# A recurrent token-mixing block on one core: square roots by ln and exp, the sigmoid by tanh, two activation tables set by the program, and a new written order

## The chip, the core and the metric

The kernel runs on one core of a Trainium2 chip. Its matrix engine is called TensorE (PE in the profile), the engine for element-wise work and scans VectorE (DVE), the one for activation functions ScalarE (ACT), the general one GpSimd (POOL); SyncE (SP) issues most transfers. ScalarE evaluates its functions from a loaded table; a function of another set of tables needs an ACT_TABLE_LOAD first. The metric is device time in microseconds, the median over runs.

## What is computed

x has 8 batches of 256 tokens with 512 channels, ctx holds the state. Shortened:

```python
xn = ln(x); sx = shift(xn) - xn                 # layer norm, token shift
xxx = tanh((xn + sx * maa_x) @ maa_w1)          # five groups of 32
x5 = xn + sx * (maa_stack + xxx @ maa_w2)       # mixes for k, w, v, r, g
w = exp(-exp(time_decay + tanh(x5[1] @ decay_w1) @ decay_w2))
r, k, v = x5[3] @ Wr.T, x5[0] @ Wk.T, x5[2] @ Wv.T
g = silu(x5[4] @ Wg.T)
# scan over tokens, 32 heads of 16 x 16:  out = r (u k v + s);  s = k v + w s
att = head_norm(out) * gn_w + gn_b              # (a - mean) * rsqrt(var + eps) per head
x = x + (att * g) @ Wo.T
xn2 = ln(x); sx2 = shift(xn2) - xn2
rr = sigmoid((xn2 + sx2 * ffn_maa_r) @ ffn_Wr.T)
kk = square(relu((xn2 + sx2 * ffn_maa_k) @ ffn_Wk.T))
x = x + rr * (kk @ ffn_Wv.T)
```

All data are float32.

## The kernel before

The program is a list of small operations, each noted with its engine, a duration, and the buffers it reads and writes (`Plan.add`). For every batch there are three stages: `inputs_of_scan` (layer norm, mixes, the products for k, w, v, r, g), `scan` (four blocks of 128 channels; each block's v is written to DRAM and read back spread over 16 rows per head, 512 KB a tile, by SP), and `rest` (head norm, gate, the Wo product, second layer norm, the two feed-forward products with weights streamed anew for each batch). Three batches are under way at a time, in different stages.

`Plan.order` sets the order of work. It takes the operations by rank from a table of numbers written out by hand (`TURNS`, one row per stage), assigns buffers from small pools as they become free, and reckons a start for each operation from the noted durations (`TAKES`, `LANDS`, `LATENCY`, `SWITCH`); the operations are then emitted sorted by these starts. Each engine works through its own part of that order strictly in sequence, and so does SP with its transfers. The PSUM pool `ps` has six buffers; `wrep`, one more, holds the decay spread out for the scans.

Places that the change and the prediction touch, with the lines of before:

- `normed` (L555 to L585): the deviation of a layer norm. With `alone` (batch 0's first norm and batch 7's second): ScalarE's Sqrt (L570) and VectorE's reciprocal (L572). Otherwise GpSimd adds eps (L561 or L580) and raises to the power -0.5 (L581), then multiplies by the negated mean (L582); ScalarE applies both (L585).
- `inputs_of_scan`: Tanh to ta (L678), the product with maa_w2's first four groups (mw2a), Tanh to tb and to w's inner value (L759, L761), Exp (L776), the product of tb with mw2b, copies of k, r and v out of PSUM (L784), Silu for g (L814).
- `scan`: Exp of the decay spread over a tile, the expansion (L859); `vs` times k (L876, on GpSimd L873), the scan (L878), its product with r on GpSimd (L881), and the sum over a head on TensorE (L889).
- `rest`: squares (L907), the product that gathers the heads' variances (L915), Sqrt on ScalarE (L920), VectorE's reciprocal (L922), 16 copies that spread the result over the rows (L944; the last batch has a product for it, L930), GpSimd's product with att (L946), ScalarE's scaling (L950), the gate (L955), the products with Wo and after (all in `mul`, L418), Sigmoid (L979) and its product with the last matmul's output (L1002, L995).

Before the work begins, 12 products of a zero tile (L476) run while the first transfers land, and one Sqrt (L479) loads its table.

## Time and profile before

| | |
|---|---|
| median of 3 runs | 613.46 us (612.87 to 613.63) |
| the profiled execution | 615.35 us, of which the span 612.9 us |
| TensorE busy | 598.5 us |
| VectorE busy | 544.3 us |
| GpSimd busy | 517.7 us |
| ScalarE busy | 510.8 us |
| table loads on ScalarE | 44 of 1.28 us |

The span runs from the first to the last instruction; the rest of an execution's time lies around it. A row of a timeline has the start, the length, the engine, the line, the operation and the tiles (out<-in), and in brackets how long the engine had been idle and whose work ended that. A matmul in float32 counts as two instructions in the trace. A row of windows has, for each engine, busy time and number of instructions, then the granted TensorE clock (1.00 is full), the share of the DMA engines and GB/s. A row of groups ends in busy time, mean ns of one, and idle time ahead.

### The profile page before, as it was taken

To read this page: it belongs to the slowest core of one execution; us is meant where nothing else is said; L and a number is where in the kernel's file an instruction comes from. 1 tells how busy PE (TensorE), PEld (TensorE's weight loads), DVE (VectorE), ACT (ScalarE), POOL (GpSimd) and SP (SyncE) were. 2 spreads that over 40 slices of the span, in tenths; PEclk is the share of its full clock that TensorE was granted. 3 is DMA by queue.
4 is the path that set the end of the run, shared out by engine and by line. 5 is a ranking of instruction groups with operands and counts; after the bars stand their busy time and mean duration, and the time that the engine had idled before them with its cause. 6 is when DMAs were issued, how large, how long until landed. Compare 5 with 4: busy or idle time off the path is not lost.

```text
span 612.9 us, 18243 instructions
## 1 busy us (share of the span) xinstructions
PE 598.5 (98%) x7592; PEld 346.8 (57%) x7592; DVE 544.3 (89%) x491; ACT 510.8 (83%) x1166; POOL 517.7 (84%) x414
## 2 busy tenths in 40 slices
PE   8999999899999999999999999999999999999997
PEld 7565555457534774367553764465644474456464
DVE  5699999999999999799898999999999999995341
ACT  4888679989899999999899898898999789955531
POOL 1789999999999898899899998899989979987030
PEclk9999999899999999999999999999999999999999
DMA  8898766758967779667877898867887986782351
GB/s 292 271 243 221 209 178 153 192 150 203 262 171 188 223 227 260 186 177 227 206 207 209 202 247 245 203 174 203 215 233 191 249 234 169 222 240 80 128 187 68
DMA packets 52497, 124.80 MB, mean 204 GB/s; under 512 B 5824, under 2 KB 11200, under 8 KB 52416
## 3 DMA queue, kind: packets, MB, share of 16 engines
q1 hardware_dynamic: 48048, 119.46, 71.4%
q10 hardware_dynamic: 4368, 4.20, 2.2%
q8 instruction: 59, 0.97, 0.7%
q14 instruction: 22, 0.18, 0.1%
HBM read 115.25 MB, written 8.39 MB: 202 GB/s over the span
## 4 chain that ended last, share of the span: by engine, by line
PE 83%; ACT 6%; POOL 4%; DVE 3%; DMA 2%; issue 1%; SPq 0%; POOLq 0%; DVEq 0%; ACTq 0%
PE ps L418 69%; PE ps L889 9%; PE ps L753 2%; PE ps L601 2%; POOL st L881 1%; DMA vo<-v 1%; DVE st L878 1%; DMA Ws<-in_wv 1%; DMA vs<-vo 1%; ACT xn L611 1%; DVE vs L876 1%; PE ps L915 1%; ACT ps L701 0%; PE ps L831 0%; ACT L859 0%
## 5 line engine op out<-in xcount | busy, mean ns | idle before, releaser
L878 DVE TENSOR_TENSOR_SCAN st<-wrep,vs 128x1024 f32<-128x1024 f32 x128 | 288.5, 2277 | 4.4 <-PE ps L889 1.6
L881 POOL TENSOR_TENSOR st<-st,r 128x1024 f32<-128x1024 f32 x128 | 254.5, 2003 | 15.1 <-DVE st L878 13.4
L876 DVE TENSOR_TENSOR vs<-vs,ps 128x1024 f32<-128x1024 f32 x122 | 144.1, 1207 | 3.2 <-ACT vs L869 2.6
L418 PE MATMUL ps<-Ws,mix 128*32 128x512 f32 (+2 forms) x864 | 114.9, 590 | 0.3 <-DVE o L1002 0.2
L418 PEld LDWEIGHTS ps<-Ws,mix 128*32 128x32 f32 (+1 forms) x864 | 37.4, 116 | 65.0 <-issue 57.5
L713 POOL TENSOR_TENSOR mix<-mix,xn 128x512 f32<-128x512 f32 x62 | 66.6, 1092 | 5.7 <-DVE mix L707 3.6
L889 PE MATMUL ps<-st,con 128*32 128x256 f32 x1024 | 62.9, 387 | 1.4 <-ACT o L979 0.8
L418 PE MATMUL ps<-mix,Wv 128*32 128x256 f32 (+1 forms) x712 | 60.0, 380 | 0.4 <-DVE mix L707 0.4
L418 PE MATMUL ps<-mix,Wk 128*32 128x256 f32 (+1 forms) x832 | 58.9, 380 | 1.1 <-DVE mix L703 1.1
L418 PE MATMUL ps<-mix,Wr 128*32 128x256 f32 (+1 forms) x664 | 59.0, 380 | 0.1
L418 PE MATMUL ps<-mix,Wg 128*32 128x256 f32 (+1 forms) x688 | 59.0, 379 | 0.0
L418 PE MATMUL ps<-mix,Ws 128*32 128x256 f32 (+1 forms) x712 | 58.3, 380 | 0.3 <-DVE att L895 0.2
L418 PE MATMUL ps<-Ws,g 128*32 128x512 f32 (+1 forms) x416 | 57.2, 597 | 0.1
L634 POOL TENSOR_TENSOR mix<-mix,xn 128x512 f32<-128x512 f32 x44 | 47.6, 1100 | 5.0 <-ACT mix L632 5.0
L418 PEld LDWEIGHTS ps<-mix,Wv 128*32 128x32 f32 (+1 forms) x712 | 39.7, 122 | 17.1 <-issue 1.7
L839 ACT COPY att<-ps 32x256 f32<-32x256 f32 x128 | 46.5, 364 | 3.1 <-PE ps L831 1.1
L418 PEld LDWEIGHTS ps<-mix,Ws 128*32 128x32 f32 (+1 forms) x712 | 39.5, 122 | 17.0 <-ACT mix L632 0.9
L418 PEld LDWEIGHTS ps<-mix,Wk 128*32 128x32 f32 (+1 forms) x832 | 37.3, 116 | 20.9 <-issue 2.0
L889 PEld LDWEIGHTS ps<-st,con 128*32 128x32 f32 x1024 | 32.7, 111 | 28.9 <-issue 5.8
L418 PEld LDWEIGHTS ps<-mix,Wr 128*32 128x32 f32 (+1 forms) x664 | 40.0, 125 | 16.0 <-issue 1.6
L418 PEld LDWEIGHTS ps<-mix,Wg 128*32 128x32 f32 (+1 forms) x688 | 39.5, 123 | 15.8 <-ACT vs L869 0.8
L701 ACT ACTIVATE ps<-ps,vec 128x256 f32<-128x256 f32 x112 | 44.6, 446 | 2.9 <-PE ps L418 2.0
(128 smaller groups left out, 961.8 us busy)
## 6 DMA issues: line engine op xcount, KB each, us to landing
vs<-vo SPq DMA_DIRECT2D x128, 512.0 KB, 5.6
Ws<-in_fk SPq DMA_DIRECT2D x16, 512.0 KB, 5.6
Ws<-in_wo SPq DMA_DIRECT2D x16, 512.0 KB, 6.8
Ws<-in_fr SPq DMA_DIRECT2D x16, 512.0 KB, 6.7
Ws<-in_fv SPq DMA_DIRECT2D x16, 512.0 KB, 5.4
x<-in_x SPq DMA_DIRECT2D x9, 512.0 KB, 7.1
vo<-v ACTq DMA_DIRECT2D x15, 256.0 KB, 4.4
out<-o SPq DMA_DIRECT2D x15, 256.0 KB, 4.6
```

What stands on the lines that cost most here:

```text
L418: nc.tensor.matmul(out[i : i + n], lhsT=w[:, i : i + n], rhs=x, start=first, stop=final)
L601: nc.tensor.transpose(ps()[:, m, n * P : (n + 1) * P], xh[n]()[:, k * P : (k + 1) * P], idt())
L611: act(256, xn, [ps, vec], lambda m=m, k=k, xn=xn, ps=ps: nc.scalar.activation(xn()[:, m, 1 : T + 1], ps()[:, m, :], AF.Identity, bias=col( ...
L634: gp(512, t, [t, xn[q]], lambda q=q, t=t: nc.gpsimd.tensor_tensor(t(), t(), xn[q]()[:, :, 1 : T + 1], ALU.add))
L701: act(256, p_, [p_, vec], lambda g=g, q=q, m=m, p_=p_: nc.scalar.activation(p_()[:, m, :], p_()[:, m, :], AF.Identity, bias=col(f"maa_{g}" ...
L713: gp(512, t, [t, xn[q]], lambda q=q, t=t: nc.gpsimd.tensor_tensor(t(), t(), xn[q]()[:, :, 1 : T + 1], ALU.add))
L753: nc.tensor.matmul(pd()[i : i + 32, 0, :], lhsT=w, rhs=src[k // 2]()[:, k % 2, :], start=(k == begin), stop=(k == end))
L839: act(350, atts[q], [pc], lambda i=32 * (2 * q + m), m=m, q=q, h=32 * h: nc.scalar.copy(atts[q]()[h : h + 32, m, :], pc()[i : i + 32, 0, :]))
L876: dve(4 * T, [vs], [vs, kp], lambda m=m, vs=vs, kp=kp: nc.vector.tensor_tensor(vs(), vs(), kp()[:, m : m + 1, :].to_broadcast([P, 4, T]), ...
L878: dve(4 * T, [st], [w, vs], lambda w=w, vs=vs, st=st: nc.vector.tensor_tensor_scan(st().rearrange("p n t -> p (n t)"), w().rearrange("p n ...
L881: gp(4 * T, st, [st, r], lambda m=m, st=st, r=r: nc.gpsimd.tensor_tensor(st(), st(), r()[:, m : m + 1, :].to_broadcast([P, 4, T]), ALU.mul ...
L889: nc.tensor.matmul(pat()[32 * i : 32 * i + 32, 0, :], lhsT=con()[:, s : s + 32], rhs=done[i]()[:, j, :], start=(j == 0), stop=(j == 3),)
```

## The change

1. Deviations. A helper `inverted` makes 1/sqrt(var + eps) on ScalarE as exp(-0.5 ln(scale var + eps)), for all layer norms: GpSimd's additions and powers, the two Sqrts and the two small reciprocals go. In `rest` the Sqrt becomes Ln and VectorE's reciprocal becomes Exp on ScalarE.
2. Sigmoid. It becomes Tanh of half the argument; the product with the last matmul's output becomes (o + 1) times it, a form with three operands, and the missing half is taken into kk by Relu with the scale sqrt(0.5).
3. Tables. The functions are sorted into two sets, "tanh" (Tanh, Silu) and "exp" (Exp, Ln). The program itself puts a load ahead of an operation of the other set as it emits the order.
4. The planner. SP's transfers no longer wait in the plan for the one issued before, those that ScalarE issues no longer take one of the eight places in flight, some VectorE operations are held until GpSimd's running one ends, and five durations are corrected.
5. New turns for all stages.

```diff
+HALF = 0.5
+TABLES = {"tanh": "silu_and_others", "exp": "natural_log_exp_and_others"}
...
-             ("ACTvo_", 0.37): 0.4}
+             ("ACTvo_", 0.37): 0.4, ("ACTsq_", 0.405): 0.49, ("PEpsm__", 0.875): 0.945, ("PEpsm__", 0.45): 0.52, ("PEpsw_", 0.875): 0.915, ("POOLvs__", 1.959): 2.25}
...
-        12 52 16 29 46 58 28 57 60 50 65 54 51 227 99 100 135 176 5 9 23 22 24 38 21 25 42 13 47 48 20 34 63,
+        11 45 15 38 49 98 95 96 109 46 94 72 220 97 55 62 64 140 16 14 26 20 27 43 18 54 58 17 40 48 19 60 61,
...
             if op.wire:
-                at = issue = max(at, issue, lanes.pop(0))
+                if op.engine == "DMA":
+                    at = max(at, lanes.pop(0))
+                    self.crossed += max(0.0, issue - at)
+                else:
+                    issue = max(at, issue)
...
+            if op.shared and began < op.end:
+                op.end = max(op.end, free["POOL"] + 0.28)
...
-    nc.scalar.activation(eh()[:, 4:6], eh()[:, 0:2], AF.Sqrt)
-    nc.gpsimd.memset(eh()[:, 2:4], -0.5)
+    nc.scalar.preload_act_table_set(TABLES["exp"])
...
+    def inverted(rs, mv, over):
+        act(2, rs, [mv, eh], lambda: nc.scalar.activation(
+            rs(), mv()[:, :, 1], AF.Ln, bias=eh()[:, 0:1], scale=over), "exp", 1)
+        act(2, rs, [rs], lambda: nc.scalar.activation(rs(), rs(), AF.Exp, scale=-0.5), "exp")
...
-            gp(2, rs, [mv], lambda: nc.gpsimd.tensor_scalar(
-                rs(), mv()[:, :, 1], 1.0 / E, EPS, ALU.mult, ALU.add), 85)
+            over = 1.0 / E
...
-        gp(2, rs, [rs, eh], lambda: nc.gpsimd.tensor_tensor(rs(), rs(), eh()[:, 2:4], ALU.pow), 340)
+            over = 1.0
+        inverted(rs, mv, over)
...
-            act(512, t, [ps], lambda t=t, ps=ps: nc.scalar.activation(t(), ps(), AF.Silu), "silu")
+            act(512, t, [ps], lambda t=t, ps=ps: nc.scalar.activation(t(), ps(), AF.Silu), "tanh")
...
         act(256, rs, [pv, eh], lambda: nc.scalar.activation(
-            rs()[:, 0:T], pv()[:, 0, :], AF.Sqrt, bias=eh()[:, 0:1]), "sqrt", 1)
-        dve(256, [rs], [rs], lambda: nc.vector.reciprocal(rs()[:, 0:T], rs()[:, 0:T]), 6.25)
+            rs()[:, 0:T], pv()[:, 0, :], AF.Ln, bias=eh()[:, 0:1]), "exp", 1)
+        act(250, rs, [rs], lambda: nc.scalar.activation(rs()[:, 0:T], rs()[:, 0:T], AF.Exp, scale=-0.5), "exp")
...
-            act(512, t, [ps], lambda t=t, ps=ps: nc.scalar.activation(t(), ps(), AF.Relu))
+            act(512, t, [ps], lambda t=t, ps=ps: nc.scalar.activation(t(), ps(), AF.Relu, scale=HALF**0.5))
...
-                o(), ps().rearrange("p m t -> p (m t)"), AF.Sigmoid), "sig")
+                o(), ps().rearrange("p m t -> p (m t)"), AF.Tanh, scale=HALF), "tanh")
...
-            dve(512, [o], [o, ps], lambda o=o, ps=ps: nc.vector.tensor_tensor(
-                o(), o(), ps().rearrange("p m t -> p (m t)"), ALU.mult))
+            dve(512, [o], [o, ps], lambda o=o, ps=ps: nc.vector.scalar_tensor_tensor(
+                o(), o(), 1.0, ps().rearrange("p m t -> p (m t)"), ALU.add, ALU.mult))
...
+            if op.engine == "ACT" and op.mode and op.mode != table:
+                table = op.mode
+                nc.scalar.preload_act_table_set(TABLES[table])
             op.emit()
```

The lines of the changed kernel lie 12 to 15 further down: L889 becomes L902, L915 L928, L920 L933, L922 L935, L930 L943, L944 L957; the loads that the program sets are at L1048. The built order has 40 loads on ScalarE (39 at L1048, one at the start) where before has 44. Of the 39, 8 stand ahead of a Silu, 5 ahead of ta, 5 ahead of tb or w's inner value, 2 ahead of rr's Tanh, 14 ahead of the expansion and 5 ahead of another Ln or Exp.

What the change moves, at three places. The first is batch 0's output stage. ScalarE's queue of before, from the root of the variances (sq_159 out of ps_169) to the first copies that spread it (rk and sq):

```order
L920 ACT_TABLE_LOAD
L920 ACTIVATE sq_159<-ps_169,eh 128x256
L869 ACTIVATE vs_145<-s_82,cm_84 128x4
L784 COPY v_129<-ps_170 128x2x256
L761 ACT_TABLE_LOAD
L761 ACTIVATE tb_121<-ps_171 64x256
L853 DMA vo_142<-v_129 128x2x256
L759 ACTIVATE w_133<-ps_171 64x256
L869 ACTIVATE vs_149<-s_82,cm_84 128x4
L944 COPY rk_150<-sq_159 32x256 x2
```

And ScalarE's queue of the changed kernel at the same place:

```order
L933 ACTIVATE sq_159<-ps_172,eh 128x256
L935 ACTIVATE sq_159<-sq_159 128x256
L957 COPY rk_150<-sq_159 32x256 x2
L957 COPY sq_158<-sq_159 32x256
L957 COPY rk_150<-sq_159 32x256 x2
L957 COPY sq_158<-sq_159 32x256 x2
L957 COPY rk_150<-sq_159 32x256
L957 COPY sq_158<-sq_159 32x256 x4
L957 COPY rk_150<-sq_159 32x256 x3
L957 COPY sq_158<-sq_159 32x256
L1048 ACT_TABLE_LOAD
L827 ACTIVATE g_136<-ps_171 128x512
```

The two loads and the work for the next batch that stood between the root and the copies now come behind all 16 copies. There follow, up to the copy of k (`L797 COPY k_123<-ps_171`), a short `vs` piece, the second Silu, the four Tanhs to tb and w with the copy of v and two `vs` pieces among them, a load and an expansion.

TensorE at the same place, before, from the gathering of the variances (L915):

```order
L915 MATMUL ps_169<-sq_159,con 32x256 x2
L915 MATMUL ps_169<-sq_158,con 32x256 x2
L418 MATMUL ps_170<-mix_111,Wv_75 32x256 x8
L418 MATMUL ps_170<-mix_117,Wv_76 32x256 x8
L753 MATMUL ps_171<-mix_115,dw_69 32x256 x2
```

and in the changed kernel:

```order
L928 MATMUL ps_172<-sq_159,con 32x256 x2
L928 MATMUL ps_172<-sq_158,con 32x256 x2
L430 MATMUL ps_174<-mix_111,Wg_79 32x256 x8
L430 MATMUL ps_174<-mix_114,Wg_80 32x256 x8
L430 MATMUL ps_172<-mix_113,Wv_75 32x256 x8
L430 MATMUL ps_172<-mix_106,Wv_76 32x256 x8
L430 MATMUL ps_171<-mix_111,Wg_79 32x256 x8
L430 MATMUL ps_171<-mix_114,Wg_80 32x256 x8
```

Two rows with x8 are one half of a product (32 instructions in the trace). Counted like this, TensorE of the changed kernel has, between the variances and the first product with Wo, five halves for g and v, the stage's product for decay and tb (L766), two halves for k, one for r, the small product of tb, the other half for r, and one sum over heads (L902). Before it has one half for v, L753, the small L831, one half for v, two for r, two for k, one for v, the small product of tb, and L889.

The second place is the start of SP's queue, the transfers from the first on. Before:

```order
L407 DMA sq_158<-in_x 128x512
L407 DMA sq_159<-in_x 128x512
L407 DMA Ws_164<-in_consts 128x128
L407 DMA Ws_165<-in_wv 128x2x512
L407 DMA idt<-in_consts 128x128
L407 DMA vec<-in_vecs 128x128
L407 DMA Ws_166<-in_wv 128x2x512
L407 DMA dw_69<-in_decay_w 128x4x64
L407 DMA mw_66<-in_maa_w 128x4x192
L407 DMA x_160<-in_x 128x2x512
L407 DMA mw2a<-in_maa_w 128x512
```

and changed:

```order
L419 DMA sq_158<-in_x 128x512
L419 DMA sq_159<-in_x 128x512
L419 DMA x_160<-in_x 128x2x512
L419 DMA idt<-in_consts 128x128
L419 DMA Ws_164<-in_wv 128x2x512
L419 DMA vec<-in_vecs 128x128
L419 DMA Ws_165<-in_consts 128x128
L419 DMA Ws_166<-in_wv 128x2x512
L419 DMA mw_66<-in_maa_w 128x4x192
L419 DMA con<-in_consts 128x448
L419 DMA Wk_74<-in_wk 128x2x512
L419 DMA mw2a<-in_maa_w 128x512
```

Batch 1's x (x_160) moves ahead of the identity, the constants and the weights; con and half of Wk move ahead of mw2a, and the decay's weights behind it.

The third place is ScalarE's queue in the last batch's head norm. Before, from the square of its last blocks:

```order
L907 ACTIVATE sq_158<-att_140 128x512
L920 ACT_TABLE_LOAD
L920 ACTIVATE sq_159<-ps_174,eh 128x256
L970 ACTIVATE mix_108<-ps_171 128x512
L814 ACT_TABLE_LOAD
L814 ACTIVATE g_136<-ps_173 128x512
```

and changed:

```order
L920 ACTIVATE sq_158<-att_140 128x512
L933 ACTIVATE sq_159<-ps_174,eh 128x256
L935 ACTIVATE sq_159<-sq_159 128x256
L1048 ACT_TABLE_LOAD
L827 ACTIVATE g_134<-ps_171 128x512
L963 ACTIVATE att_138<-att_138,vec 128x256 x2
L963 ACTIVATE att_140<-att_140,vec 128x256 x2
L827 ACTIVATE g_136<-ps_170 128x512
```

The load ahead of the root is gone, the reciprocal has become the row behind it, and one more Silu comes behind the root.

## The prediction

> **What bounds the kernel now.** I read the page's busy shares first, then TensorE's waits, then the timelines of the engines where TensorE waits longest, then the start and the end of the span. The page's first part:

> ```profile
> span 612.9 us, 18243 instructions
> PE 598.5 (98%) x7592; PEld 346.8 (57%) x7592; DVE 544.3 (89%) x491; ACT 510.8 (83%) x1166; POOL 517.7 (84%) x414
> ```

> TensorE (PE) is busy for 598.5 of 612.9 us. No edit removes a matrix product, so work taken off VectorE, GpSimd or ScalarE is worth time only where TensorE waits for it. TensorE's waits (us in total, times, longest):

> ```profile
> PE ps L418 <- ACT k L784: 2.1, 1, 2.1
> PE ps L418 <- DMA Ws<-in_wv: 1.2, 1, 1.2
> PE ps L418 <- DVE mix L703: 1.1, 1, 1.1
> PE ps L476 <- DVE hm L474: 1.0, 1, 1.0
> PE ps L601 <- ACT xh L585: 0.9, 1, 0.9
> PE ps L930 <- ACT g L814: 0.9, 1, 0.9
> PE ps L889 <- ACT o L979: 0.8, 1, 0.8
> ...
> PE ps L889 <- POOL st L881: 0.2, 1, 0.2
> ```

> The seven on top make 8.0 us, and seven more of 0.4 to 0.2 us are left below. Two of the seven (the weights' landing and the first memset, 2.2 us) belong to the start of the program. So waits that this change could touch hold some 6 us, plus what they drag behind them. The longest does drag something. TensorE's timeline around it, in the middle of batch 0's output stage:

> ```profile
> 99.39 0.61 PE L915 MATMUL ps<-sq,con 128*32 128x256 f32 x8
> ...
> 116.30 0.69 PE L418 MATMUL ps<-tb,mw2b 32*64 32x256 f32 x16 [2.06 <-ACT k L784]
> 117.37 3.27 PE L889 MATMUL ps<-st,con 128*32 128x256 f32 x32 [0.37 <-ACT v L784]
> 120.34 4.09 PE L418 MATMUL ps<-Ws,g 128*32 128x512 f32 x32
> ```

> and the granted clock there (the column before the last two):

> ```profile
> 118.00:120.00 2.00, 2.00 (x26) 1.22 (x22) 1.15 (x3) 1.97 (x8) 2.00 (x3) 0.50 1.03 238
> 120.00:122.00 2.00, 2.00 (x20) 0.79 (x16) 1.36 (x1) 1.91 (x7) 2.00 (x2) 0.69 1.03 222
> ```

> After 2.06 and 0.37 us of waiting the clock is halved. It runs at 0.50 for 2 us and at 0.69 for 2 more, which is 1.0 + 0.6 = 1.6 us of lost work. This one place costs 2.06 + 0.37 + 1.6 = 4.0 us, the largest single loss behind the start.

> **The change, part by part.** *Batch 0's output stage.* Between the product that gathers the variances (L915) and the first product with Wo (120.34) lies a chain over ScalarE, VectorE and GpSimd:

> ```profile
> 100.11 1.28 ACT L920 ACT_TABLE_LOAD   x1
> 102.56 1.28 ACT L761 ACT_TABLE_LOAD   x1
> 104.84 0.82 ACT L944 COPY rk<-sq 32x256 f32<-32x256 f32 x2
> 111.06 0.40 ACT L944 COPY rk<-sq 32x256 f32<-32x256 f32 x1
> 115.69 0.56 ACT L784 COPY k<-ps 128x512 f32<-128x512 f32 x1
> 102.93 1.73 DVE L922 RECIPROCAL sq<-sq 128x256 f32<-128x256 f32 x1
> 109.10 3.95 POOL L881 TENSOR_TENSOR st<-st,r 128x1024 f32<-128x1024 f32 x2
> ```

> A load for Sqrt, the Sqrt, the wait for VectorE, the reciprocal (1.73), and only then 16 copies from 104.84 to 111.46. GpSimd's product then waits behind two scans' products until 113.05, ScalarE's scaling waits for GpSimd, and the copy of k, whose PSUM buffer TensorE wants, stands behind that scaling until 115.69. The change puts Ln and Exp in place of load, Sqrt and reciprocal. Ln is priced as the Sqrt row below, 0.47; Exp over 256 columns as the tanh of the same width (L678).

> ```profile
> L920 ACT ACTIVATE sq<-ps,eh 128x256 f32<-128x256 f32 x8 | 3.8, 474 | 0.1
> L678 ACT ACTIVATE ta<-ps 128x256 f32<-128x256 f32 x8 | 3.0, 379 | 2.3 <-PE ps L418 2.3
> 97.85 1.73 PE ps L418 x32
> ```

> The product ends at 100.0; Ln and Exp end at about 101.05; so the copies start 3.8 us sooner and, with no other work among them in the new order, end near 107.7. Behind them, up to and with the copy of k, the new ScalarE order has two loads (2.6 us), two Silus (0.60 each, as the one at 567.50 below), four Tanhs (0.38 each), two copies (0.56 each) and an expansion of the decay with a few short pieces, 1.3 us as an estimate: 7.7 us, so the copy starts near 115.4 and k is out near 116.0. TensorE's cover grows too: between the variances and the first Wo product the new order has nine pieces of 1.73 us (the last row above, a piece of the chain), one of 3.45 and two small ones, 19.9 us, where before had 16.9. It reaches tb's product near 115.6 and waits some 0.4 us; the gate for Wo is ready near 120.2, where TensorE arrives at 119.9. Bounds: all of the 4.0 us goes, or none. I take 3.3 us off, since the chain and its cover come out even, and waits of 0.3 or 0.4 us are far from the 2 us after which the clock fell.

> [...]

> *The last batch's end.* The same chain, where nothing else fills in:

> ```profile
> 563.93 1.28 ACT L920 ACT_TABLE_LOAD   x1 [1.11 <-PE ps L915]
> 565.73 1.75 DVE L922 RECIPROCAL sq<-sq 128x256 f32<-128x256 f32 x1 [3.58 <-ACT sq L920]
> 567.50 0.60 ACT L814 ACTIVATE g<-ps 128x512 f32<-128x512 f32 x1
> 568.15 1.13 PE L930 MATMUL ps<-sq,con 64*128 64x256 f32 x8 [0.90 <-ACT g L814]
> ```

> L930 needs the reciprocal (567.48) and a PSUM buffer that the Silu frees at 568.10. With no load (the order keeps Exp's set) Ln and Exp are done near 564.9, and the new order writes L930's output into the buffers of the variances and of the last scan, free by then. TensorE's 1.73 us of filling ends at 565.4, so the 0.90 us goes, with 0.2 us around it: 1.1 us. Bounds: 0 and 1.3. Late next is the last gate: one load, two Silus and four scalings end near 570.5, and the filling behind L930 lasts until 571.4.

> *The start.* The transfers change places. Rows of before:

> ```profile
> 0.00:20.00 20.00, 16.46 (x151) 14.57 (x152) 13.50 (x31) 10.85 (x23) 3.90 (x18) 1.00 0.92 313
> 5.74 0.87 SPq L407 DMA_DIRECT2D mw2a<-in_maa_w  x1
> mw2a<-in_maa_w SPq DMA_DIRECT2D x1, 256.0 KB, 7.2
> 7.38 0.29 ACT L604 COPY xn<-vec 128x2 f32<-128x2 f32 x2 [1.92 <-DMA vec<-in_vecs]
> ```

> The queue is full (0.92 of the engines, 313 GB/s), so what is put ahead delays what follows. Batch 1's x (512 KB) goes ahead of vec, and the 64 KB of centring constants behind it: 448 KB more, 1.4 us at 313 GB/s. vec, waited for until 7.38 now, then lands near 8.8, and xn can't start sooner. mw2a has 608 KB more ahead of it, so it lands not at 5.74 + 7.2 = 12.9 but near 14.9, and its product, now at 13.77, starts 1.1 us later:

> ```profile
> 13.77 1.12 PE L418 MATMUL ps<-ta,mw2a 32*64 32x256 f32 x32
> ```

> Against it stands that batch 1's statistics and scaling run earlier, in time that VectorE idles away now (TensorE waits 0.9 us for xh L585). I take 0.5 us of loss, between a gain of 0.9 and a loss of 1.9.

> *Engines off the path.* The small powers go from GpSimd and the reciprocals from VectorE; ScalarE gets Ln and Exp on two columns (priced as the Sqrt on two, 296 ns) and has 40 loads for 44, as the two orders count them:

> ```profile
> L581 POOL TENSOR_TENSOR rs<-rs,eh 128x2 f32<-128x2 f32 x14 | 9.8, 700 | 0.9
> L570 ACT ACTIVATE rs<-mv,eh 128x2 f32<-128x2 f32 x2 | 0.6, 296 | 8.2 <-DVE mv L568 8.2
> L859 ACT ACT_TABLE_LOAD x11 | 14.1, 1283 | 0.2
> L707 DVE SCALAR_TENSOR_TENSOR mix<-ps,vec,sx 128x256 f32<-128x256 f32 x12 | 5.1, 477 | 1.1 <-PE ps L418 1.1
> L736 DVE TENSOR_TENSOR mix<-ps,sx 128x256 f32<-128x256 f32 x28 | 11.0, 411 | 1.3 <-ACT ps L734 1.2
> ```

> GpSimd loses at least the 9.8 us of L581. VectorE loses eight reciprocals, 8 x 1.73 = 13.8 us, and gains about 2: the product with rr becomes a three-operand form, 66 ns dearer per 256 columns by the last two rows, so 0.13 us for each of 15. ScalarE loses 4 x 1.28 = 5.1 us and gains about 8 x 0.38 + 30 x 0.3 = 12 us at most, so it goes from 511 to some 518 us of 613. TensorE's 598.5 us covers all three, so I cost this at nothing; without that cover ScalarE's 7 us would be the price. At the very end two products on VectorE cost 0.07 us more each, of which one shows.

> [...]

> *The new turns elsewhere.* Every other wait of TensorE, 1.1 us and below, belongs to the old order. I assume that the new order has about as many of its own: 0, with 3 us either way.

> Sum: -3.3 - 1.1 + 0.5 = -3.9 us. The profiled execution took 615.35 us, of which 612.9 is the span; it becomes 611.4. It lies 1.9 us above the median of the three timed runs (613.46), so the forecast is 613.46 - 3.9 = 609.6 us.

> **The rivals.** *All waits go.* With VectorE and GpSimd each over 10 us lighter, the new order may close nearly all of them: the 6 us of touchable waits on top, 1.6 us of half clock and some of the 2 us below, 8 to 9 us: 604.9. For it speaks that both engines are over 80% busy now; against it that all waits but one are short already, and the start gets no better.

> *Given back.* The wait for k stays over 2 us, because two loads stand ahead of its copy in the new order, and the clock still falls; only the end gains, and the start takes half of it: 612.9, no change.

> *Slower: Exp and Tanh no longer share a set.* Before, one load served tanh, both exponentials and the expansion; the loads stood ahead of Silu, Sqrt and Sigmoid (11, 8 and 8) and of the expansion (11). In the new order five loads stand ahead of ta, five ahead of tb or w, and 14 ahead of the expansion. ScalarE works its queue in order, so each holds up PSUM evacuations by 1.28 us. A load that hits a moment with no spare PSUM buffer, as at 116.30, costs 4.0 us with its half clock. Three such places instead of one: 613.46 + 8.0 - 0.6 (end and start as summed) = 620.9; two instead of one: 616.9. It decides from the point where TensorE's wait passes 2 us. Against it: 28 us of loads ahead of Silu and the expansion (22 x 1.28) stand in the old queue, and only one such place shows. [...]

> That the change doesn't do what it says can be ruled out: the built order has 39 loads at the new line, one at the start and none elsewhere.

> **How the numbers follow.** The forecast 609.6 (606.5 to 612.0 by its own bounds) gets 0.50, all waits gone 0.20, given back 0.16, slower 0.14. A measurement here can tell 0.2%, 1.2 us, from no change. Faster than 612.2: 0.50 and 0.20, and 0.02 of the third case: 0.72. Within 612.2 to 614.7: 0.14. Slower: 0.14. The range goes from 604.0, below all waits gone, to 614.5, which takes in the third case; outside lie the slower case and the far end of the second.

> **What would show it.** Right: no half clock between 5 us and the last 3 us; a TensorE wait below 1 us ahead of tb's product in batch 0; no wait ahead of the last batch's selecting product (now L943); mw2a's first product near 14.9. Wrong: a wait above 2 us with a load on ScalarE ahead of the copy it waits for; a clock of 0.50 in the middle; VectorE or GpSimd busier than before; the start over 2 us later.

## The result and the profile after

| | kernel before | changed kernel | ratio, 95% interval |
|---|---|---|---|
| first timing, medians of 4 runs | 613.33 us (612.87 to 613.63) | 608.80 us (608.56 to 609.41) | 0.9920 (0.9903 to 0.9936) |
| second timing (with e5), 16 and 6 runs | 614.01 us (612.68 to 619.37) | 608.40 us (608.13 to 609.66) | 0.9899 (0.9875 to 0.9922) |
| profiled execution, its span | 615.35 us, 612.9 us | 608.87 us, 607.1 us | |

The change makes the kernel 4.5 us faster (5.6 us in the second timing); the forecast was 3.9 us. The two spans differ by 5.8 us, more than the medians, because the profiled execution of before was 2.0 us longer than its median and that of the changed kernel lies at its median.

The first part of the page of the changed kernel, engine by engine:

```profile
span 607.1 us, 18838 instructions
PE 597.6 (98%) x7892; PEld 344.4 (57%) x7892; DVE 531.2 (87%) x481; ACT 513.3 (85%) x1199; POOL 505.4 (83%) x385
```

VectorE is 13.1 us lighter, GpSimd 12.3, ScalarE 2.5 heavier, TensorE as busy as before within 0.9 us. So the time came out of TensorE's idle time and its clock, not out of its work. Its waits in the changed kernel (us in total, times, longest):

```profile
PE ps L488 <- DVE hm L486: 1.1, 1, 1.1
PE ps L614 <- DMA idt<-in_consts: 1.0, 1, 1.0
PE ps L430 <- DMA Ws<-in_consts: 0.7, 1, 0.7
PE ps L614 <- DVE xh L588: 0.5, 1, 0.5
PE ps L430 <- DVE mix L716: 0.4, 1, 0.4
PE ps L430 <- ACT k L797: 0.3, 1, 0.3
...
```

Six of 0.2 us follow. The twelve make 5.2 us, where fourteen made 9.9. The three on top belong to the start of the program, as two of before's did. The 2.1 us for k became 0.3, and the 1.1 (mix L703 before), 0.9 (g L814) and 0.8 us (o L979) are 0.4, nothing and 0.2.

Batch 0's output stage on ScalarE (start, us, line, tile) and then on TensorE:

```profile
95.79 0.63 ACT L920 ACTIVATE sq<-att 128x512 f32<-128x512 f32 x1 [0.60 <-DVE att L908]
...
97.15 0.47 ACT L933 ACTIVATE sq<-ps,eh 128x256 f32<-128x256 f32 x1
97.66 0.42 ACT L935 ACTIVATE sq<-sq 128x256 f32<-128x256 f32 x1
98.16 0.81 ACT L957 COPY rk<-sq 32x256 f32<-32x256 f32 x2
...
112.29 0.58 ACT L797 COPY k<-ps 128x512 f32<-128x512 f32 x1
```

```profile
96.72 0.39 PE L928 MATMUL ps<-sq,con 128*32 128x256 f32 x2
...
112.93 0.69 PE L430 MATMUL ps<-tb,mw2b 32*64 32x256 f32 x16 [0.28 <-ACT k L797]
...
117.03 5.33 PE L430 MATMUL ps<-Ws,g 128*32 128x512 f32 x48
```

and the granted clock in the 4 us in which it had fallen to 0.50 and 0.69 before:

```profile
118.00:120.00 2.00, 2.00 (x24) 0.54 (x19) 2.00 (x3) 1.94 (x7) 2.00 (x2) 1.00 0.50 175
120.00:122.00 2.00, 2.00 (x24) 0.65 (x20) 2.00 (x2) 1.91 (x7) 2.00 (x2) 1.00 0.88 223
```

No load and no reciprocal stand ahead of the copies of the reciprocals; there is a wait of 0.28 us in place of 2.06, none ahead of Wo, and the clock at 1.00.

### The profile page after: what moved, and what is told of

It reads as the page before. It is cut to its first block, busy times and chain, and to the rows that moved or that the text cites. A ratio compares the mean times of both kernels' runs of the same rounds, so it can differ in the third digit from the quotient of the medians.

```text
span 607.1 us, 18838 instructions
## 1 busy us (share of the span) xinstructions
PE 597.6 (98%) x7892; PEld 344.4 (57%) x7892; DVE 531.2 (87%) x481; ACT 513.3 (85%) x1199; POOL 505.4 (83%) x385
## 4 chain that ended last, share of the span: by engine, by line
PE 88%; ACT 6%; DMA 4%; DVE 2%; issue 1%; SPq 0%; DVEq 0%; ACTq 0%
PE ps L430 73%; PE ps L902 9%; PE ps L614 2%; PE ps L766 2%; DMA Wk<-in_wk 2%; ACT ps L714 1%; DMA mw2a<-in_maa_w 1%; ACT sq L957 1%; DMA x<-in_x 1%; PE ps L928 1%; ACT L1048 1%; PE ps L844 1%; ACT rk L957 1%; ACT mix L984 0%; DVE x L974 0%
## 5 line engine op out<-in xcount | busy, mean ns | idle before, releaser
L894 POOL TENSOR_TENSOR st<-st,r 128x1024 f32<-128x1024 f32 x128 | 254.2, 2002 | 11.3 <-DVE st L891 10.4
L889 DVE TENSOR_TENSOR vs<-vs,ps 128x1024 f32<-128x1024 f32 x122 | 144.6, 1208 | 9.3 <-ACT vs L882 6.5
L430 PEld LDWEIGHTS ps<-Ws,mix 128*32 128x32 f32 (+1 forms) x804 | 38.8, 118 | 62.7 <-issue 55.6
L902 PE MATMUL ps<-st,con 128*32 128x256 f32 x1024 | 62.6, 380 | 0.3 <-DVE x L974 0.2
L1048 ACT ACT_TABLE_LOAD x39 | 50.0, 1283 | 1.1 <-ACT v L797 0.4
L430 PEld LDWEIGHTS ps<-mix,Wv 128*32 128x32 f32 (+1 forms) x832 | 37.9, 116 | 19.5 <-issue 1.1
L902 PEld LDWEIGHTS ps<-st,con 128*32 128x32 f32 x1024 | 34.1, 110 | 26.3 <-issue 5.1
L430 PEld LDWEIGHTS ps<-mix,Ws 128*32 128x32 f32 (+1 forms) x784 | 39.6, 118 | 16.4 <-DVE mix L640 0.6
## 6 DMA issues: line engine op xcount, KB each, us to landing
vo<-v ACTq DMA_DIRECT2D x15, 256.0 KB, 4.9
out<-o SPq DMA_DIRECT2D x15, 256.0 KB, 4.6
```

The costliest lines, as they stand in the source:

```text
L430: nc.tensor.matmul(out[i : i + n], lhsT=w[:, i : i + n], rhs=x, start=first, stop=final)
L889: dve(4 * T, [vs], [vs, kp], lambda m=m, vs=vs, kp=kp: nc.vector.tensor_tensor(vs(), vs(), kp()[:, m : m + 1, :].to_broadcast([P, 4, T]), ...
L894: gp(4 * T, st, [st, r], lambda m=m, st=st, r=r: nc.gpsimd.tensor_tensor(st(), st(), r()[:, m : m + 1, :].to_broadcast([P, 4, T]), ALU.mul ...
L902: nc.tensor.matmul(pat()[32 * i : 32 * i + 32, 0, :], lhsT=con()[:, s : s + 32], rhs=done[i]()[:, j, :], start=(j == 0), stop=(j == 3),)
L1048: nc.scalar.preload_act_table_set(TABLES[table])
```

## The experiments

Each kernel was timed beside the kernel before on the same chip. "Added" below is what a kernel takes above the changed kernel, each set against before's median beside it: 614.22 us for e1 to e4, 614.01 for e5 to e8 (the changed kernel is 5.6 below that), 614.76 for e9 to e12. It is uncertain by some 2 us, as the intervals show, since the executions of one kernel spread by 1 to 7 us.

| run | median us | ratio to before, 95% interval | added us |
|---|---|---|---|
| e5 changed kernel again | 608.40 | 0.9899 (0.9875 to 0.9922) | 0 |
| e6 old head norm, batch 0 | 611.75 | 0.9949 (0.9928 to 0.9970) | 3.3 |
| e7 old head norm, last batch | 609.70 | 0.9921 (0.9897 to 0.9944) | 1.3 |
| e1 old head norm, all batches | 631.78 | 1.0281 (1.0255 to 1.0307) | 23.2 |
| e9 old layer norms | 618.76 | 1.0072 (1.0049 to 1.0094) | 9.6 |
| e10 old Sigmoid | 625.56 | 1.0193 (1.0163 to 1.0224) | 16.4 |
| e12 all three old | 657.86 | 1.0703 (1.0679 to 1.0727) | 48.7 |
| e2 kernel before, new turns | 669.31 | 1.0892 (1.0857 to 1.0926) | 60.7 |
| e3 changed kernel, old turns | 651.89 | 1.0609 (1.0582 to 1.0637) | 43.3 |
| e4 start: x behind mw2a | 615.92 | 1.0021 (1.0005 to 1.0036) | 7.3 |
| e11 start: idt and vec sooner | 609.01 | 0.9908 (0.9887 to 0.9929) | -0.1 |
| e8 a load ahead of k's copy | 609.95 | 0.9930 (0.9904 to 0.9955) | 1.6 |

**The yardstick.** No edit.

> The changed kernel unchanged, as the yardstick of the others beside it: 608 to 610, no half clock in the middle of the span.

Measured 608.40 us, with no half clock between the start and the end.

**The old head norm in one place.** The order of all other instructions is the changed kernel's; e6 has `b == 0`, e7 `last`, e1 neither condition:

```diff
+        if b == 0:
+            sq_op, re_op = plan.stages[-1][-2:]
+            sq_op.own, re_op.own = "sqrt", None
+            sq_op.emit = lambda: nc.scalar.activation(rs()[:, 0:T], pv()[:, 0, :], AF.Sqrt, bias=eh()[:, 0:1])
+            re_op.emit = lambda: nc.vector.reciprocal(rs()[:, 0:T], rs()[:, 0:T])
...
-            if op.engine == "ACT" and op.mode and op.mode != table:
+            use = getattr(op, "own", op.mode)
+            if op.engine == "ACT" and use and use != table:
```

> The changed kernel, order kept, with the old head norm (load, Sqrt, reciprocal) in batch 0 alone. Theory A (the forecast's first term: the chain's length sets TensorE's stall there): as in the run with all eight, the copies start 2.0 us later, at 100.1 in place of 98.16, and TensorE waits 2.4 us more ahead of the Silu's and k's buffers: 611 to 612.5. Theory B (what was lost with all eight came from the batches behind): below 609.8. If the clock halves as in the kernel before, up to 1.6 us more.

> The same for the last batch alone. Theory A (the forecast's second term): the selecting product waits 1.0 us for the reciprocal, 1.1 us in all: 609.9. Theory B (the filling behind it takes it up): 608.8, with the wait moved to the gate ahead of Wo.

e6 took 611.75 us, inside theory A's range. ScalarE's and TensorE's rows of it:

```profile
96.35 0.63 ACT L920 ACTIVATE sq<-att 128x512 f32<-128x512 f32 x1 [0.74 <-DVE att L908]
...
97.59 1.28 ACT L1054 ACT_TABLE_LOAD   x1
...
101.59 0.82 ACT L962 COPY rk<-sq 32x256 f32<-32x256 f32 x2 [2.24 <-DVE sq L940]
```

```profile
110.27 3.66 PE L430 MATMUL ps<-mix,Wk 128*32 128x256 f32 x64 [1.93 <-ACT g L827]
116.37 0.69 PE L430 MATMUL ps<-tb,mw2b 32*64 32x256 f32 x16 [0.71 <-ACT k L797]
```

Counted from the squares (L920, at 95.79 in the changed kernel), the copies start 5.24 us later here and 2.37 there, tb's product 20.02 and 17.14: the chain is 2.9 us longer, and TensorE is 2.9 us behind. Of that 1.93 + 0.71 - 0.28 = 2.4 us show as waits for buffers. The expectation's 2.0 us for the copies compared absolute times of two executions and was too small for that reason. The clock stays at 1.00. e7 took 609.70 us (609.51 to 610.99, against 608.13 to 609.66 on the same chip), and the wait stands where it was expected:

```profile
562.79 1.13 PE L948 MATMUL ps<-sq,con 64*128 64x256 f32 x8 [0.98 <-DVE sq L940]
```

In the new order the short chain is worth 3.3 and 1.3 us at the two places; the second is near what these intervals can tell, and its wait of 0.98 us is the firmer number. The 3.3 us hold no half clock, unlike the loss of before.

**The old head norm everywhere.**

> The changed kernel with its order kept instruction by instruction; only the head norm of all eight batches is made as before: load for Sqrt, Sqrt on ScalarE, reciprocal on VectorE (11 loads more). Theory A (the gain is the shorter chain of Ln and Exp at the two places where TensorE waited): the wait ahead of tb's product in batch 0 comes back, 0.3 us -> over 1.5 us, and the last batch's selecting product waits some 1 us again; the time goes from 608.8 to 612 to 614. Theory B (the gain is the new order and its cover of 21.2 us between the variances and Wo in batch 0, and the chain has slack): below 610.5, with no wait over 1 us in batch 0's output stage.

Theory A has the direction, but its number was 612 to 614, and the run took 631.78: the six batches between cost 18.6 us more, some 3 us each. TensorE's largest waits in it ("issue" is idle time for which the profile shows no cause):

```profile
PE ps L430 <- issue: 3.1, 2, 2.8
PE ps L430 <- ACT k L797: 2.8, 2, 2.1
```

So the new order counts on the short chain in every batch, though before's order waited for the long one in batch 0 and at the end only. Theory B is out. Part of the 23.2 us is half clock: the six timed executions were granted 0.995 of it in the mean, which is 3 us of 630.

**The other old ways, one by one and together.** e9 and e10 keep the order too; e12 has e1, e9 and e10 at once.

```diff
+            first.emit = lambda: nc.gpsimd.tensor_scalar(rs(), mv()[:, :, 1], over, EPS, ALU.mult, ALU.add)
+            second.emit = lambda: nc.gpsimd.tensor_tensor(rs(), rs(), eh()[:, 2:4], ALU.pow)
```

```diff
-                o(), ps().rearrange("p m t -> p (m t)"), AF.Tanh, scale=HALF), "tanh")
+                o(), ps().rearrange("p m t -> p (m t)"), AF.Sigmoid), "tanh")
+            plan.stages[-1][-1].own = "sigmoid"
...
-            dve(512, [o], [o, ps], lambda o=o, ps=ps: nc.vector.scalar_tensor_tensor(
-                o(), o(), 1.0, ps().rearrange("p m t -> p (m t)"), ALU.add, ALU.mult))
+            dve(512, [o], [o, ps], lambda o=o, ps=ps: nc.vector.tensor_tensor(
+                o(), o(), ps().rearrange("p m t -> p (m t)"), ALU.mult))
```

> The changed kernel, order kept, but the 14 layer norms that share their engines with other batches make their deviations on GpSimd again (the product and sum 195 ns, the power 700 ns, in place of Ln 293 and Exp 198 ns on ScalarE); the first and the last norm keep Ln and Exp. The forecast's fourth term (engines off the path cost nothing): within 0.6 us of the changed kernel's 608.4, GpSimd 12 us busier. Rival (the new order counts on the shorter chain, as it does with the head norm): over 610, with waits of TensorE for xh.

> The changed kernel, order kept, with the gate of the second half by Sigmoid from its own set and a plain product, as before: 13 table loads more (16.7 us of ScalarE). The fourth term again (loads lie off the path): 608.4 to 609.2. Rival of the forecast (a load ahead of an evacuation costs): each load that falls into a place without slack costs up to 1.3 us, some of the 13 do: 611 to 617.

> The changed kernel's order, kept instruction by instruction, with all the old ways at once: head norm by Sqrt and reciprocal, 14 layer norms on GpSimd, gate by Sigmoid. Theory A (each old way costs for itself where the new order has no slack): the sum of the three single runs, 631.8 + what the runs with layer norms and with Sigmoid add. Theory B (one late chain makes slack for the next): below that sum by 3 us or more. It also tells whether the kernel before with the new turns (669.3) is slow by its operations or because its planner, with other costs, sorts the same turns into another order: near 669 says operations, below 645 says sorting.

e9 and e10 went to the rivals. e9 takes 618.76 us. By its durations the chain is 0.4 us longer (0.19 + 0.70 for 0.29 + 0.20), but it now stands in GpSimd's queue behind the products with r, and ScalarE waits for it. ScalarE's largest wait in e9, and the same wait in e5, the changed kernel:

```profile
ACT xh L604 <- POOL nm L601: 12.9, 10, 2.0
```

```profile
ACT xh L598 <- POOL nm L595: 1.5, 4, 0.5
```

One of the ten, on ScalarE and, 5 us later, on TensorE, for a copy of r that stands behind it in ScalarE's queue:

```profile
205.10 1.52 ACT L604 ACTIVATE xh<-x,nm,rs 128x512 f32<-128x512 f32 x2 [1.87 <-POOL nm L601]
```

```profile
210.19 3.66 PE L430 MATMUL ps<-mix,Wk 128*32 128x256 f32 x64 [1.17 <-ACT r L803]
```

e10 takes 625.56 us for 13 loads more, 1.26 us in the mean for each load of 1.28. That is not the loads' length alone: two spells of half clock, 1.7 us each, are in its trace. TensorE's largest wait is for a buffer that the Sigmoid frees:

```profile
PE ps L430 <- ACT o L992: 6.1, 3, 3.6
```

e12 takes 48.7 us more than the changed kernel; e1, e9 and e10 alone add 23.2 + 9.6 + 16.4 = 49.2. The three sum within the uncertainty, theory A. In the new order none of the three edits is off TensorE's path.

**Operations and turns crossed.**

```diff
-        12 52 16 29 46 58 28 57 60 50 65 54 51 227 99 100 135 176 5 9 23 22 24 38 21 25 42 13 47 48 20 34 63,
+        11 45 15 38 49 98 95 96 109 46 94 72 220 97 55 62 64 140 16 14 26 20 27 43 18 54 58 17 40 48 19 60 61,
...
```

(The first row of the table in e2, the kernel before with all rows of the changed kernel's table; e3 is the other way round.)

> The kernel before, with its own operations and planner's rules, but the changed kernel's table of turns. Theory A (the operations make the gain): about as slow as before, 612 to 615, with a wait over 1.5 us somewhere in batch 0's output stage. Theory B (the order makes it): 608.5 to 610.5.

> The changed kernel's operations and table sets with the turns of before. The old turns mix exponentials and tanh, which no longer share a set: 73 table loads behind the start in place of 39, so 34 x 1.28 = 43.6 us more on ScalarE, 557 of some 610 us busy. Theory A (shorter chain wins wherever it stands): no more than 612. The rival of the prediction (each load ahead of an evacuation that TensorE waits for costs it): 616 or more, with several waits of TensorE for ScalarE over 1 us.

Neither theory foresaw 669.31 and 651.89. First rows of TensorE's waits, e2 and then e3:

```profile
PE ps L601 <- ACT xh L585: 7.7, 5, 3.4
PE ps L418 <- POOL st L881: 5.7, 1, 5.7
```

```profile
PE ps L430 <- ACT w L772: 5.4, 3, 3.1
PE ps L430 <- ACT k L797: 4.6, 1, 4.6
```

New operations with old turns are 38 us slower than before, and old operations with new turns 55 us slower, while new with new is 5.6 us faster. So "operations or order" has no answer here: each table of turns does well with its own operations alone. (The planner's new rules went with the operations in both runs; what they do by themselves was not tried.) Of e2's 60.7 us the old operations in the fixed order explain 48.7 (e12). Of the other 12 us some 8 are half clock: e2's timed executions were granted 0.979 of the clock in the mean and e12's 0.991, an estimated loss of 14 and 6 us. What makes e2 wait longer (the planner sorts the same turns with other costs; the two lone norms) wasn't taken apart. In e3 the loads are 73 in place of 39 and ScalarE is the engine that TensorE waits for most, which is the forecast's slower rival, made true by the old turns; five spells of half clock (8.5 us) are in its 43.3 us. How much of the 43.3 us the 34 loads more make is not shown, since much else differs in e3 too; the new turns batch the functions by their two sets and have 39.

**The start.**

```diff
-        for op in plan.order(phases):
+        done = plan.order(phases)
+        first = ["xt0_0", "xt0_1", "idt", "Wraw0", "vec", "cen", "Wraw1", "mw1", "mw2a", "xt1", "con", "Wk1"]
+        at = [i for i, op in enumerate(done) if op.engine == "DMA"][: len(first)]
+        lot = {done[i].bufs[0].name: done[i] for i in at}
+        for i, name in zip(at, first):
+            done[i] = lot[name]
+        for op in done:
```

(e4; e11 has "idt", "xt1", "vec", "cen", "Wraw0" behind the two pieces of batch 0's x, and mw2a last as in the changed kernel.)

> The changed kernel with the first twelve transfers of the queue in another order: batch 1's x (512 KB) behind mw2a in place of ahead of idt, and idt ahead of Wv's first half; all else in place. Theory of the prediction (vec and mw2a land later in the changed kernel, which costs 0.5 us): vec's copy 1.4 us sooner, mw2a's first product near 13.5 in place of 14.74, and the time 0.5 us less, 608.3. Rival: batch 1's statistics, which the new order has early on VectorE, now wait for their x and take it back: 608.8 to 610.

> The changed kernel with idt ahead of batch 1's x, and vec and the centring constants right behind that x, ahead of Wv's first half; so that x stays ahead of everything large. Theory from the run in which x stood behind mw2a (VectorE's queue stops at batch 1's statistics when that x is late, the 64 KB transfers are late by the megabyte ahead of them): idt's wait 0.9 us goes below 0.6, vec's copy comes at 8.3 in place of 9.0, the time 0.4 us less than 608.4. Rival: batch 1's x lands 0.2 us later and its statistics hold VectorE up by as much: no difference.

e4 is 7.3 us slower, far beyond both expectations. Its VectorE row and its TensorE row:

```profile
DVE st L582 <- DMA x<-in_x: 5.8, 1, 5.8
```

```profile
17.14 3.75 PE L430 MATMUL ps<-mix,mw 128*128 128x256 f32 x8 [6.66 <-DVE mix L640]
```

vec came sooner (its copy at 7.19 for 9.00), but in VectorE's new queue batch 1's statistics stand ahead of batch 0's scaling, and they wait 5.8 us for batch 1's x. The early transfer of that x, which the forecast booked as a loss, is what this queue needs. Of the 7.3 us 3.4 are clock: behind the wait it stays at 0.50 for 6.83 us. e11 keeps it early and has vec's copy at 7.52, but now Wv's half comes last:

```profile
9.14 1.13 PE L430 MATMUL ps<-Ws,Ws 128*128 128x128 f32 x8 [1.23 <-DMA Ws<-in_wv]
```

609.01 us, -0.1 us by the table, is no difference: the rival's number. Its cause is there only in part: VectorE now waits 0.41 us for batch 1's x, and the 1.23 us for Wv are a wait that neither theory had.

**One load more ahead of k's copy.**

```diff
+            if op.engine == "ACT" and op.bufs[0].name == "k2_1" and op.kind == "ACTk_":
+                for _ in range(2):
+                    nc.scalar.preload_act_table_set(TABLES[table])
```

> The changed kernel with two more loads of the same table set on ScalarE (2.57 us) just ahead of the copy of k that TensorE waits for in batch 0's output stage (0.28 us now). The forecast's reading of the kernel before, for which a wait past 2 us halves the clock: the wait becomes 2.8 us, the clock falls to 0.5 for some 3.4 us behind it, and the time grows by 2.6 + 1.6 = 4.2 us, to 613. Rival (the half clock needs a longer wait or more waits together): 2.6 us or less, at 611.4, with the clock at 1.00.

Only one of the two loads is in the trace, so the edit was half as large as meant. ScalarE's and TensorE's rows:

```profile
111.98 1.28 ACT L1051 ACT_TABLE_LOAD   x1
```

```profile
113.92 0.69 PE L430 MATMUL ps<-tb,mw2b 32*64 32x256 f32 x16 [1.57 <-ACT k L797]
```

The wait grew from 0.28 to 1.57 us, by the load's 1.28, and the time by 1.6; the clock stayed at 1.00. It doesn't test the point at which the clock falls; the fourteen traces together do (last section).

## Why the prediction came out, and where not

**Batch 0's output stage: -3.3 us.** The mechanism held step by step; the size is in part luck. Counted from the end of the variances' product (its last two pieces end at 97.1 here, at 100.0 before), the copies of the reciprocals end after 7.7 us (7.7 forecast), k is out after 15.8 (16.0), tb's product starts after 15.8 and waits 0.28 us (16.0 and 0.4), Wo starts after 19.9 without a wait (its gate was forecast for 20.2, TensorE for 19.9). One of these agreements comes out of a slip: the 7.7 us of work "up to and with the copy of k" held that copy already, and the forecast added its 0.6 us once more to get from 115.4 to 116.0. By its own sum k was due after 15.4 us; the work took 8.1 us in place of 7.7.

The term is 3.0 us in the trace by the count below (100 to 140 us): 2.2 us less idle time and 1.7 us of half clock gone, with 0.8 us of small losses inside products against them. e6 undoes it for 3.3 us, but without any half clock, so that the two 3.3 agree by chance. The half clock itself was no fixed cost: of 44 timed executions of the kernel before, 26 were granted 0.997 of the clock or less and 18 0.999 or more (the changed kernel's ten: all 0.999 or more), and the medians of the first kind are some 1 us longer. The forecast took its 1.6 us from one execution that had it. It also didn't have the 1.6 us of small losses in the 20 us ahead (0.3 us of them idle time), so that the stage as a whole gained 1.4.

**The last batch's end: -1.1 us.** 1.0 us by the same count, 1.3 us in e7. TensorE at the end of the changed kernel:

```profile
560.76 1.13 PE L943 MATMUL ps<-sq,con 64*128 64x256 f32 x8
...
578.01 1.09 PE L614 MATMUL ps<-idt,xh 128*128 128x128 f32 x8 [0.46 <-DVE xh L588]
```

No wait stands ahead of L943, and none ahead of Wo at 567.08, 8.6 us behind the variances' product for 9.5 before. What is late next is the last layer norm, 0.46 us, which the forecast didn't name.

**The start: +0.5 us.** Rows of TensorE and of ScalarE:

```profile
7.52 1.06 PE L614 MATMUL ps<-idt,xh 128*128 128x128 f32 x8 [0.97 <-DMA idt<-in_consts]
...
14.74 1.12 PE L430 MATMUL ps<-ta,mw2a 32*64 32x256 f32 x32
```

```profile
9.00 0.20 ACT L617 COPY xn<-vec 128x2 f32<-128x2 f32 x1 [2.86 <-DMA vec<-in_vecs]
```

vec at 9.0 (8.8 forecast), mw2a's product at 14.74 (14.9), 0.5 us lost by 40 us. The places are right. The size is not shown: the same count gives 0.0 in e5, the changed kernel again, and 0.9 in e6, whose start is the same. That the early x is also a need of the new order (e4) was not in the forecast.

**Engines off the path: 0.** Two sizes were off. Rows of the changed kernel, and the old product's row of before:

```profile
L1015 DVE SCALAR_TENSOR_TENSOR o<-o,ps 128x512 f32<-128x512 f32 x15 | 10.2, 679 | 17.7 <-PE ps L430 17.6
L558 ACT ACTIVATE rs<-rs 128x2 f32<-128x2 f32 x16 | 3.2, 198 | 0.3
```

```profile
L1002 DVE TENSOR_TENSOR o<-o,ps 128x512 f32<-128x512 f32 x15 | 10.2, 680 | 4.6 <-PE ps L418 4.6
```

The three-operand product costs what the plain one did, 679 and 680 ns, not 0.13 us more; ScalarE grew by 2.5 us, not 7. What failed is the reading behind the zero: "TensorE's 598.5 us covers all three". It covers the busy time of an engine, not the length of a chain. e9 and e10 put 9.6 and 16.4 us on the path by giving such work back in this order. The forecast's zero could stand because its question was the sum of a new order, in which this work is gone, and not for the reason that it gave.

**The new turns elsewhere: 0 with 3 us either way.** This term came out negative. To see it, count TensorE's lost time: the length of a stretch less what its matmuls take in an unbroken product (1.73 us for 32 pieces of 256 columns, and so by columns for the other shapes; the warm-up counts as lost). It is worked out from all of TensorE's rows. One trace stands on each side, so a few tenths of a microsecond mean nothing.

| stretch, us | lost before | lost after | difference |
|---|---|---|---|
| 0 to 40 | 11.3 | 11.8 | +0.5 |
| 40 to 80 | 4.1 | 1.7 | -2.4 |
| 80 to 100 | 0.7 | 2.3 | +1.6 |
| 100 to 140 | 5.0 | 2.0 | -3.0 |
| 140 to 300 | 5.4 | 4.1 | -1.3 |
| 300 to 560 | 5.9 | 5.7 | -0.2 |
| 560 to the end | 6.2 | 5.2 | -1.0 |
| sum | 38.6 | 32.9 | -5.8 |

The three terms that had a mechanism (0 to 40, 100 to 140, 560 on) make -3.5 us of -5.8. The rest, -2.3 us, came from places that were put at 0: before's wait of 1.1 us for mix L703 and the small ones around it, and 0.8 us for o L979, less 1.6 us of new small losses ahead of the variances. If the three terms are taken as counted here, it is -1.0 by the medians (-4.5 us) and -2.1 by the second timing's (-5.6). So the two large terms hold, and the sum of 3.9 fell short of the measured 4.5 by this term, within its 3 us. Why just these waits went in the new order was not tried by itself.

**The rivals.** "All waits go" was not reached: 2.8 us stay at the start, and 2.4 us in nine waits behind it. "Given back" didn't happen: two loads do stand ahead of k's copy, at 104.80 and 109.94 us, but the wait is 0.28. "Slower" is real as a price: one load ahead of k's copy lengthened TensorE's wait by 1.3 us (e8), and the 13 of e10 cost as much each in the mean, half clock included. The new turns avoid it by their batching (39 loads for 73, e3).

## What to carry to other kernels

When an order is fitted to its durations, the stall that a change removes can be forecast place by place from the old trace, but the worth of an operation cannot be read by putting the old one back in the new order: here that costs 49 us, about ten times the gain. Change operations and order together, and judge by the pair. A busy engine under another's cover is no proof of slack: ask for the chain that runs through it, and for what stands ahead in its queue (batch 1's statistics at the start, e4).

## What the runs showed of the hardware

In these runs the half clock went with where a wait lay, not with its length alone. In the fourteen traces (before, changed, e1 to e12) all half-clock spells between the start-up and the last 4 us of a span last 3.41 or 6.83 us at 0.50, so each costs 1.7 or 3.4 us. Of TensorE's waits over 1 us (without the one of 1.03 to 1.05 us at each program's start):

| wait | half clock within 4 us | full clock |
|---|---|---|
| 2.12 us and longer (to 6.66) | 16 | 0 |
| 2.05 to 2.07 us | 4 | 4 |
| 1.01 to 1.99 us | 4 | 41 |

(One of the four in the last line came 1.1 us behind a wait of 2.06 us and shares its spell.) The stall of the kernel before was one of the eight at the edge.

So two waits of the same 2.06 us can differ. In e2 the wait lies within one piece, which has 3.41 - 1.35 = 2.06 us of idle time, and the clock fell; in e1 a border cuts it, the piece has 1.60 us and the next 0.66, and the clock stayed. e1's row, then the pieces and their successors of e2 and of e1 (TensorE's busy time is the second number, the clock the column before the last two):

```profile
168.19 1.12 PE L430 MATMUL ps<-ta,mw2a 32*64 32x256 f32 x32 [2.06 <-ACT ta L691]
```

```profile
564.62:568.03 3.41, 1.35 (x24) 0.60 (x20) 3.41 (x3) 3.31 (x9) 2.62 (x2) 1.00 0.21 46
568.03:571.45 3.42, 3.42 (x40) 1.74 (x33) 3.42 (x3) 3.35 (x6) 2.78 (x4) 0.50 1.02 301
```

```profile
164.31:167.73 3.42, 1.82 (x20) 0.37 (x12) 3.42 (x4) 3.12 (x5) 3.22 (x3) 1.00 0.64 156
167.73:171.14 3.41, 2.75 (x48) 1.15 (x52) 2.23 (x2) 3.29 (x10) 2.00 (x1) 1.00 0.58 145
```

In the kernel before the piece from 114.40 to 117.81 us held 1.90 us of the wait of 2.06 and the 0.37 us behind it, 2.28 us in all (3.41 less 1.13 busy); the longer wait alone would have stayed below the 1.940 us. The most idle time in any other piece of that trace, short of its end, is 1.31 us (from 15.41 us), and in the changed kernel 1.70 us (from 6.51 us); behind both the clock stayed at 1.00. So the forecast's "2 us after which the clock fell" is near the measured 1.94, but in these traces the fall went with the idle time within one piece, not with the length of one wait: in before two waits added up to it, and by the same figure a border could split even a wait of up to twice 1.94 us so that the clock stays (an estimate; no wait over 2.07 us was split so). Where the grid lies differs from trace to trace (5.17 and 6.51 us above), so by the four and four of the table the forecast's 1.6 us were a chance of about one in two at 2.06 us.
